# Perceiver block on Trainium2: GpSimd takes part of the closing sums, shared sums come earlier, the last load is cut in two

## The chip, the core and the metric

The kernel runs on one core of a Trainium2 chip (trn2). The metric is the device time of one execution in microseconds (us); the median of several runs counts. Beside it there is one profiled execution with its trace, from which all durations of single instructions come. The engines are named as in the profile: PE (TensorE, matmuls; PEld is its weight load), DVE (VectorE), ACT (ScalarE), POOL (GpSimd) and SP (SyncE, which here issues most DMAs).

## What is computed

x is a tensor of 64 sequences of 32 rows with 256 features: 2048 rows. Six residual layers follow each other: windowed cross-attention to a context, causal self-attention, a quantised linear layer, full cross-attention, a gated mixer with a short convolution, and a mixture of experts. Only the end of the last one matters here. Cut to that:

```python
flat = layernorm(x).reshape(2048, 256)
probs = softmax(flat @ router_w + router_b)              # 8 experts
topk_probs, topk_idx = top_k(probs, 2)                    # two experts per row
shared_out = gelu(flat @ sw1 + sb1) @ sw2 + sb2
h1 = gelu(einsum('td,edh->teh', flat, rw1) + rb1)
expert_out = einsum('teh,ehd->ted', h1, rw2) + rb2
out = x + shared_out + sum over the two chosen e of topk_probs[t, e] * expert_out[t, e]
```

## The kernel before

x stays in SBUF in four tiles `x0` to `x3`, one for each group g of 512 rows. A group has NT = 4 subtiles t of 128 rows, so a tile is 128 partitions x 4 x 256 numbers (float32). The tiles collect the residual sum in place, and the result is stored from them.

`mixture()` (line 1621) does the last layer. It routes the rows, and runs 20 turns over tiles of rows sorted by expert: POOL gathers rows of y by an indirect DMA (`gather`, line 1815), PE and ACT compute the hidden layer, PE the output, DVE adds the expert's bias, and POOL scatters the result by an indirect DMA to a DRAM buffer `r_rows` (`outputs`, line 1948, the DMA at line 1964). `r_rows` holds, for both choices `which` of each row, that expert's output in the row's own place.

After the last scatter the closing stage begins (line 2015 onward):

- **Loads.** SP loads `r_rows` back in eight DMAs of 512 KB, in the order g = 0..3, and within a group `which` = 0, 1 (lines 2020 to 2022). They wait for the last scatters.
- **Weights.** `weigh(g)` (line 2033): ACT multiplies subtiles of r in place by the routing weights `pw`, one instruction of 128x256 each. `by_scalar` (line 2028) says which subtiles ACT takes: all four for `which` = 1; for `which` = 0 only t = 2 and 3, but all four in group 3; and none of the last load (g = 3, `which` = 1).
- **Sums.** `sum_up(g)` (line 2039): where ACT has scaled, DVE adds two subtiles of r to x in one `tensor_tensor` of 128x512. Elsewhere DVE multiplies and adds in one `scalar_tensor_tensor` of 128x256 per subtile. After the second choice of a pair of subtiles, SP issues the store of this pair, 256 KB: eight stores in all.
- **The shared expert.** `fill_outputs(n)` (line 1115, which steps through `shared_outputs`, line 1068) lets PE compute the shared expert's output for n subtiles into PSUM, and `settle()` (line 1089) lets DVE add what is ready to x, a pair of subtiles (128x512) at a time. The results `ps_so` alternate between two PSUM banks, so the matmuls of a pair wait until DVE has read the pair before the last one. At the start of the closing stage four pairs are left: both of group 2 and both of group 3.

Engines take their instructions in program order, and the order of the closing stage is this:

```python
        for g in range(NG):
            weigh(g)
        fill_outputs(2)
        settle()
        sum_up(0)
        for g in range(1, NG):
            fill_outputs(2)
            settle()
            sum_up(g)
```

So one shared pair is settled ahead of each group's sums: group 2's first pair ahead of group 0's sums, group 2's second ahead of group 1's, group 3's first ahead of group 2's, and group 3's second ahead of group 3's own. POOL has nothing to do in this stage after its last scatter. All instructions issued through the helper of line 107 bear that line in the profile; matmuls bear line 119.

The functions:

Of the kernel before, what the change touches and what calls it, by code (L numbers as in the profile page):

```python
# [12 lines left out]
ALU = mybir.AluOpType  # L13
# [7 lines left out]
NG, NT = 4, 4  # L21
# [44 lines left out]
def perceiver_kernel(ctx: ExitStack, tc: tile.TileContext, a: dict, out: bass.AP):  # L66
# [32 lines left out]
    class InOrder:  # L99
# [12 lines left out]
    vector, scalar, gpsimd, sync = (  # L112
        InOrder(e) for e in (nc.vector, nc.scalar, nc.gpsimd, nc.sync)
    )
# [974 lines left out]
    def settle(n=None):  # L1089
        for _ in range(len(owed) if n is None else n):  # L1090
            owed.pop(0)()

    def by_halves(unit, places):
        places = iter(places)
        begun = []

        def fill(n):
            left = round(2 * n)
            while left:
                if begun:  # L1100
                    finish(begun.pop())
                    left -= 1
                    continue
                half = unit(*next(places), left == 1)
                next(half)
                if left == 1:
                    begun.append(half)
                else:
                    finish(half)
                left -= min(left, 2)  # L1110

        return fill

    fill_hidden = by_halves(shared_hidden, [(g, c) for g in range(NG) for c in range(4)])
    fill_outputs = by_halves(shared_outputs, [(g, t) for g in range(NG) for t in range(NT)])
# [505 lines left out]
    def mixture():  # L1621
# [393 lines left out]
        r_view = r_rows[: 2 * NB * S].rearrange("(w g t p) d -> g p w t d", w=2, g=NG, p=P)  # L2015
        whole = sb.tile([P, 4, NT, D], F32, tag="kb0", name="r")
        r = [(whole[:, 0], whole[:, 1]), (whole[:, 2], whole[:, 3])]
        r_ = ring(sb, *wide[0:4])
        r += [tuple(r_([P, NT, D], "r") for _ in range(2)) for _ in range(2)]
        for g in range(NG):  # L2020
            for which in range(2):
                sync.dma_start(out=r[g][which], in_=r_view[g, :, which])

        def weight(g, which, t):
            at = which * nt + g * NT + t
            return pw[:, at : at + 1]

        def by_scalar(g, which):
            if g == NG - 1 and which == 1:
                return ()  # L2030
            return range(NT) if which or g == NG - 1 else range(2, NT)

        def weigh(g):
            for which in range(2):
                for t in by_scalar(g, which):
                    rows_t = r[g][which][:, t, :]
                    scalar.activation(rows_t, rows_t, AF.Copy, scale=weight(g, which, t))

        def sum_up(g):
            for which in range(2):  # L2040
                for t0 in range(0, NT, 2):
                    if t0 in by_scalar(g, which):
                        x = xs[g][:, t0 : t0 + 2, :]
                        vector.tensor_tensor(x, x, r[g][which][:, t0 : t0 + 2, :], ALU.add)
                    else:
                        for t in range(t0, t0 + 2):
                            x = xs[g][:, t, :]
                            vector.scalar_tensor_tensor(
                                x, r[g][which][:, t, :], weight(g, which, t), x, ALU.mult, ALU.add
                            )  # L2050
                    if which == 1:
                        sync.dma_start(
                            out=out_view[g][:, t0 : t0 + 2], in_=xs[g][:, t0 : t0 + 2]
                        )

        for g in range(NG):
            weigh(g)
        fill_outputs(2)
        settle()
        sum_up(0)  # L2060
        for g in range(1, NG):
            fill_outputs(2)
            settle()
            sum_up(g)

    out_view = out.rearrange("(g t p) d -> g p t d", g=NG, p=P)
    mixture()
    attention.close()

# [151 lines left out]
```

## Time and profile before

| what | value |
|---|---|
| median of 3 runs | 887.53 us (887.43 to 887.73) |
| the profiled execution | 888.15 us, its span 886.4 us |
| PE busy in the span | 851.0 us (96%) |
| DVE, ACT, POOL busy | 576.1, 438.5, 513.9 us |
| first load of r issued | 865.41 us into the span |
| last instruction of DVE ends | 883.15 us |
| closing stage, from the first load to the end | 21.0 us |
| plain adds x<-x,r on DVE | 11 of 128x512, 685 ns mean |
| weighted adds x<-r,w,x on DVE | 10 of 128x256, 478 ns mean |
| shared sums x<-ps_so,x on DVE in the stage | 4 of 128x512, 685 ns mean |
| scalings r<-r,w on ACT | 22 of 128x256, 496 ns mean |

Times in the trace are counted from the span's start. A group of instructions bears a mean duration; consecutive instructions on one engine overlap a little, so the distance from start to start is shorter than the duration. DMAs appear twice: as an issue on SP's queue, and as packets on the 16 DMA engines. The chain of waits follows instructions on engines; it ends with the last of these, and a transfer that lands after it is not part of it.

### The profile page before, as it was taken

What the parts mean: (1) busy time and instruction counts of PE and PEld (TensorE: products, weight loads), DVE (VectorE), ACT (ScalarE), POOL (GpSimd) and SP (SyncE); (2) the same over time, 40 slices, a digit from 0 to 9 for tenths busy, and PEclk for the clock granted to TensorE, in tenths of its full rate; (3) what the DMA queues carried; (4) which work ended last, traced back from release to release, by engine and by line L of the source; (5) the groups of instructions that cost most, each with busy time, mean ns of one, the idle gap of its engine ahead of it and who ended that gap; (6) DMA issues with size and microseconds to landing.
All of it is one profiled execution on the core that took longest, in us unless ns stands there. A gap on an engine that the chain in (4) does not pass through costs nothing. (4 is left out here: it accounts for less than half of the span.)

```text
span 886.4 us, 22890 instructions
## 1 busy us (share of the span) xinstructions
PE 851.0 (96%) x8729; PEld 586.9 (66%) x8729; DVE 576.1 (65%) x1692; ACT 438.5 (49%) x1135; POOL 513.9 (58%) x1004
## 2 busy tenths in 40 slices
PE   7989999999999999999999999999999999999995
PEld 3566666665466666666666665666667568888894
DVE  6888777896777576885778756866766861111116
ACT  2756667674654555565445645575652323222224
POOL 4677777785774657575575754685651254555430
PEclk9999999999999999999999999999999999999999
DMA  6564433553110111110111101120010046777768
GB/s 216 146 164 119 120 92 96 143 138 104 54 55 24 34 54 55 55 55 2 55 54 56 55 1 55 55 73 25 3 36 2 24 169 219 232 232 232 220 191 290
DMA packets 66926, 88.77 MB, mean 100 GB/s; under 512 B 32480, under 2 KB 50688, under 8 KB 64768
## 3 DMA queue, kind: packets, MB, share of 16 engines
q1 hardware_dynamic: 62592, 76.95, 28.9%
q0 software_dynamic: 3456, 9.44, 3.2%
q8 instruction: 69, 1.13, 0.5%
q10 hardware_dynamic: 768, 0.92, 0.4%
q14 instruction: 41, 0.34, 0.1%
HBM read 65.78 MB, written 13.11 MB: 89 GB/s over the span
## 5 line engine op out<-in xcount | busy, mean ns | idle before, releaser
L107 ACT ACTIVATE e<-e,xnm 128x257 f32<-128x257 f32 x256 | 127.2, 499 | 43.7 <-DVE xnm L107 40.4
L119 PE MATMUL ps_k<-ct,w_w_l1x 128*128 128x512 f32 x256 | 122.8, 602 | 1.1 <-ACT yT L107 0.5
L107 POOL TENSOR_SCALAR e<-e,xsm 128x256 f32<-128x256 f32 x256 | 123.4, 500 | 0.0
L107 DVE CUSTOM_DVE_ANT_0 e<-ps_s,mask 128x257 f32<-128x257 f32 x256 | 93.5, 421 | 43.3 <-PE ps_s L119 43.1
L119 PE MATMUL ps_v<-w_w_l1x,ct 128*128 128x256 f32 x512 | 121.1, 379 | 0.0
L122 PE MATMUL ps_t<-cst,e 128*128 128x128 f32 x640 | 101.7, 281 | 2.3 <-DVE eT L107 2.0
L119 PEld LDWEIGHTS ps_v<-w_w_l1x,ct 128*128 128x128 f32 x512 | 93.4, 190 | 10.8 <-ACT y L107 0.2
L107 DVE COPY eT<-ps_t 128x512 f32<-128x512 f32 x124 | 85.1, 686 | 23.4 <-PE ps_t L122 23.3
L107 ACT ACTIVATE kT<-ps_k,vec 128x512 f32<-128x512 f32 x64 | 44.0, 687 | 97.9 <-PE ps_k L119 96.4
L107 POOL TENSOR_TENSOR x<-x,rows 128x256 f32<-128x256 f32 x96 | 70.0, 747 | 28.2 <-DVE y L107 24.9
L107 ACT ACTIVATE hTr<-ps_h,w 128x256 f32<-128x256 f32 (+1 forms) x80 | 31.4, 450 | 110.3 <-issue 89.4
L122 PEld LDWEIGHTS ps_t<-cst,e 128*128 128x128 f32 x640 | 71.4, 140 | 20.1 <-DVE eT L107 4.8
L107 DVE TENSOR_TENSOR og<-ps_o,b 128x512 f32<-128x512 f32 (+1 forms) x20 | 12.8, 638 | 105.6 <-PE ps_o L119 105.6
L119 PEld LDWEIGHTS ps_k<-ct,w_w_l1x 128*128 128x128 f32 x256 | 44.6, 190 | 42.0 <-issue 34.1
L1964 POOL DMA_INDIRECT r_rows<-og,lv x36 | 35.5, 986 | 60.8 <-DVE og L107 55.9
L119 PE MATMUL ps_h<-ygT,w 128*128 128x256 f32 (+1 forms) x320 | 67.2, 364 | 0.0
L107 ACT COPY v<-ps_v 128x512 f32<-128x512 f32 x80 | 46.4, 581 | 41.1 <-PE ps_v L119 40.7
L107 POOL TENSOR_TENSOR last<-e,xsm 128x4 f32<-128x4 f32 x64 | 15.3, 238 | 88.6 <-DVE xsm L107 87.1
L119 PE MATMUL ps_o<-w,hTr 128*128 128x256 f32 x288 | 65.3, 379 | 0.0
L119 PEld LDWEIGHTS ps_h<-ygT,w 128*128 128x128 f32 x320 | 56.0, 194 | 6.4 <-issue 0.2
L119 PEld LDWEIGHTS ps_o<-w,hTr 128*128 128x128 f32 x288 | 54.4, 190 | 7.2
L107 ACT ACTIVATE kb<-kT,cst 128x256 f32<-128x256 f32 x96 | 45.4, 512 | 23.8 <-POOL kT L107 23.7
(225 smaller groups left out, 1671.4 us busy)
## 6 DMA issues: line engine op xcount, KB each, us to landing
ct<-in_ctxT SPq DMA_DIRECT2D x16, 1024.0 KB
w<-in_ew SPq DMA_DIRECT2D x20, 514.0 KB
w<-in_ew SPq DMA_DIRECT2D x20, 512.0 KB
far<-part SPq DMA_DIRECT2D x126, 64.0 KB
v_rows<-v SPq DMA_DIRECT2D x16, 256.0 KB
vb<-v_rows SPq DMA_DIRECT2D x64, 64.0 KB
r<-r_rows SPq DMA_DIRECT2D x8, 512.0 KB
b<-in_eb SPq DMA_DIRECT2D x20, 128.0 KB
```

Of the source, the lines that this page charges most:

```text
L107: ins = getattr(self.engine, name)(*args, **kw)
L119: return kept(nc.tensor.matmul(ps, **args))
L122: return kept(nc.tensor.transpose(ps, src, eye))
L1964: wrote = nc.gpsimd.indirect_dma_start(out=r_rows, out_offset=bass.IndirectOffsetOnAxis(ap=write_i[:, at : at + 1], axis=0), in_=o[:, i, : ...
```

## The change

```diff
         for g in range(NG):
             for which in range(2):
-                sync.dma_start(out=r[g][which], in_=r_view[g, :, which])
+                for t0 in range(0, NT, 2 if g == NG - 1 and which == 1 else NT):
+                    ts = slice(t0, t0 + 2) if g == NG - 1 and which == 1 else slice(0, NT)
+                    sync.dma_start(out=r[g][which][:, ts], in_=r_view[g, :, which, ts])
...
                     if t0 in by_scalar(g, which):
                         x = xs[g][:, t0 : t0 + 2, :]
-                        vector.tensor_tensor(x, x, r[g][which][:, t0 : t0 + 2, :], ALU.add)
+                        eng = gpsimd if which == 0 and t0 == 2 else vector
+                        eng.tensor_tensor(x, x, r[g][which][:, t0 : t0 + 2, :], ALU.add)
...
         for g in range(NG):
             weigh(g)
-        fill_outputs(2)
+        fill_outputs(4)
         settle()
-        sum_up(0)
-        for g in range(1, NG):
-            fill_outputs(2)
-            settle()
+        for g in range(NG):
             sum_up(g)
+            if g < 2:
+                fill_outputs(2)
+                settle()
```

Three things are in it.

1. In each group, the plain add of the first choice's subtiles 2 and 3 (128x512) moves from DVE to POOL: four adds. DVE's add of the second choice to the same subtiles now waits for POOL. In group 3, where the second choice is not scaled by ACT, it is the weighted add of subtile 2 that waits.
2. Both shared pairs of group 2 are now settled ahead of group 0's sums, group 3's first pair after group 0's sums, and group 3's second pair after group 1's. The order of PE's matmuls stays as it was.
3. The last load (g = 3, `which` = 1) becomes two loads of 256 KB, of subtiles 0 and 1 and of subtiles 2 and 3. SP issues nine loads and then the eight stores as before. The weighted adds of subtiles 0 and 1 need only the first half.

On DVE four instructions fewer are issued, on POOL four more, on SP one more; ACT and PE have the same.

## The prediction

> **What bounds the end now.** Only the last 25 us of 886.4 are touched, so I read the chain of waits for that stretch first, then the timeline of VectorE (DVE), ScalarE (ACT) and the DMA issues, then the busy time by stages.
>
> ```profile
> by line: DVE x L107 0.5%; issue 0.1%; DVEq L2217 0.0%; DVEq L107 0.0%
> ...
> 880.88 1.08 DVE x L107 x2
> 881.96 0.40 DVEq L2217
> 882.36 0.79 DVE x L107 x2
> ```
>
> The chain says "DVE, adds into x", up to 883.15. But the span ends at 886.4: 3.2 us follow that the chain does not show.
>
> ```profile
> 865.41 6.98 SPq L107 DMA_DIRECT2D r<-r_rows  x8
> ...
> 872.61 10.94 SPq L107 DMA_DIRECT2D out<-x  x8
> ...
> 876.70 3.38 ACT L107 ACTIVATE r<-r,w 128x256 f32<-128x256 f32 x8 [0.30 <-DMA r<-r_rows]
> 877.09 0.87 DVE L107 SCALAR_TENSOR_TENSOR x<-r,w,x 128x256 f32<-128x256 f32 x2
> 877.88 1.89 DVE L107 TENSOR_TENSOR x<-x,r 128x512 f32<-128x512 f32 x3
> 879.68 0.68 DVE L107 TENSOR_TENSOR x<-ps_so,x 128x512 f32<-128x512 f32 x1
> 880.28 1.28 DVE L107 TENSOR_TENSOR x<-x,r 128x512 f32<-128x512 f32 x2
> 881.49 1.67 DVE L107 SCALAR_TENSOR_TENSOR x<-r,w,x 128x256 f32<-128x256 f32 x4
> ```
>
> DVE works without a gap to 883.15. A 128x512 add follows the next after 0.60 us (1.89 for three is 2 x 0.60 + 0.69), a weighted 128x256 add after 0.39.
>
> ```profile
> 868.00:872.00 4.00, 4.00 (x20) 3.53 (x19) 1.69 (x4) 1.96 (x5) 0.00 (x0) 1.00 1.10 365
> ...
> 876.00:880.00 4.00, 1.75 (x9) 1.19 (x7) 4.00 (x8) 3.70 (x9) 0.00 (x0) 1.00 1.09 367
> 880.00:882.00 2.00, 0.00 (x0) 0.00 (x0) 2.00 (x5) 0.08 (x1) 0.00 (x0) 0.99 1.09 384
> ...
> 883.00:884.00 1.00, 0.00 (x0) 0.00 (x0) 0.15 (x1) 0.00 (x0) 0.00 (x0) 0.50 0.75 249
> ```
>
> The last two columns are the DMA engines' busy share and GB/s: full from 868 to 882, with a dip only at 883. So there is a second bound, nearly as late as DVE. By the DMA queue's completions in the trace, the eight loads of r land from 869.36 to 879.78, about 1.5 us apart, and the eight stores at 880.42, 881.08, 881.71, 882.38, 883.04, 883.72, 884.55, 885.32. The first store was issued at 872.61 and landed at 880.42, just behind the last load: the queue works in order, 0.66 us per store. Only the last two stores wait for DVE: the eighth was issued at 883.18 and landed 2.14 us later. The program's end follows 1.05 us after that.
>
> **The floor.** If DVE were infinitely fast, stores 7 and 8 would follow the sixth at 0.66 each: 883.72 + 1.32 = 885.04, against 885.32. Whatever is taken off DVE can gain 0.28 us, 0.03% of the time. More is not to be had unless the loads get faster.
>
> **The change, part by part.**
>
> (1) *Four 128x512 adds leave DVE*: 4 x 0.60 = 2.40 us off its queue. This is the gross gain, of which the floor lets 0.28 through.
>
> (2) *They go to GpSimd (POOL).* Its row for such an add:
>
> ```profile
> L107 POOL TENSOR_TENSOR near<-near,cst x28: 1269/1278/1301, 29.2 to 187.5; 128x512 f32<-128x512 f32 x28
> ```
>
> So 1.27 us each, starting 0.08 after ACT's last scaling (the smallest gap in these rows). POOL's last scatter, queued ahead, ends at 863.83. ACT finishes the scaled pair at 870.35 (group 0), 873.45, 876.40 and 880.08 (group 3). Undisturbed, the adds are done at 871.7, 874.8, 877.75 and 881.43. The DVE add that waits for each comes at 872.68, about 875.6, 878.4; these waits cost nothing. In group 3 the weighted add of tiles 2 and 3 must wait for 881.43.
>
> (3) *The adds do not run beside DVE for free.* Early in this trace:
>
> ```profile
> 20.93 0.15 DVE L107 TENSOR_TENSOR sq<-r 128x4 f32<-128x4 f32 x1
> 21.09 1.26 POOL L107 TENSOR_TENSOR kT<-near,far 128x512 f32<-128x512 f32 x1 [0.40 <-DVE sq L107]
> 21.11 1.26 DVE L107 SCALAR_TENSOR_TENSOR sq<-sq,ve 128x4 f32<-128x4 f32 x1
> ...
> 22.41 0.16 DVE L107 SCALAR_TENSOR_TENSOR rn<-sq,r 128x4 f32<-128x4 f32 x1
> ```
>
> A 4-column operation of DVE, worth 0.16, took 1.26: it stood still while POOL added. With operations of the size in question:
>
> ```profile
> 688.36 1.58 POOL L107 TENSOR_TENSOR x<-x,rows 128x256 f32<-128x256 f32 x2 [0.71 <-ACT y L107]
> 688.53 1.69 DVE L107 SCALAR_TENSOR_TENSOR conv<-yT,vec,conv 128x248 f32<-128x248 f32 x2
> ```
>
> Each of these two weighted adds ended 0.27 after the POOL add beside it (690.22 against 689.94), where alone it takes 0.48. Both operands of these DVE operations lie in SBUF, as in the adds into x. The shared sums read PSUM; rows of that kind (part from ps_qk, ps_x into x) keep their 0.75 and 0.68 beside POOL, so I let them run.
>
> The Trainium skill, SBUF — State Buffer, section "Who interferes with whom", says that a VectorE instruction with two SBUF inputs and a GpSimd instruction that reads SBUF exclude each other, and that the second "fully blocks" until the first finishes. The 0.27 above is softer than this at the seam: by the rule the sum below would be +0.78, by the row -0.18.
>
> Now the DVE queue of the changed program, in its order, with the row's 0.27:
> - Shared sums ahead: group 2's second one at 869.06 (its matmuls end then), so the first weighted adds begin at 869.66, not 869.38. It is recovered at once: the next DVE add waits for ACT until 871.88, as before. Group 0's POOL add (870.5 to 871.75) lies in that gap.
> - Group 1: POOL 873.53 to 874.80. The two weighted adds, due at 873.89, end at 875.07 and 875.46; plain adds start at 875.38 and 875.98, the last shared sum at 876.58. Its matmuls follow group 3's first ones without the 1.55 us that TensorE waited at 874.03, and end by 875.9.
> - Group 2: POOL gets in at 876.6, to 877.87. Weighted adds end at 878.14 and 878.53; plain adds at 878.45 and 879.05; group 3's one plain add at 879.65.
> - Group 3: POOL 880.25 to 881.52. The weighted adds end at 881.79, 882.18, 882.57 and 882.96; if DVE's first of them gets ahead of POOL, the end is the same within 0.05.
>
> The eighth store goes out at 883.00, not 883.18: it lands at 885.14, the floor being 885.04. Of the 2.40 us, group 1 gives back 0.7, group 2 0.5, group 3 1.1: this is where the gain goes.
>
> (4) *The last load in two halves.* Same bytes. One more issue on SP: an issue of a load took 0.39 to 1.4 us there, mostly held by the full queue; it delays the first store's issue, which has no way to move before 879.8 anyway. The first half lands some 0.7 us ahead of 879.78, so at 879.1: group 3's first weighted adds are free from then, but DVE is there at 880.25 in any case. Worth nothing; at worst a gap of 0.1 between halves, at best stores' pace (0.66 per half instead of 0.74), 0.15. No wait of SP is new on the path: each store also waits for a load's landing, now one load later, and the eighth for the second half at 879.8, long past.
>
> The Trainium skill, DMA: Bandwidth & Descriptors, section "Anatomy of one DMA — SWDGE (gpsimd) path", gives each DMA about 2.0 us of fixed cost beside its bytes. Paid in sequence, that would put the second half and every store 2 us later, 889.5 in all; the stores' spacing of 0.66 in this trace speaks against it.
>
> **Sum.** Profiled execution: 888.15 in all, span 886.4; the median of the runs shown is 887.53, and I apply the difference to that. 887.53 - 0.18 = **887.35 us**.
>
> **Rivals.**
> - *Full exclusion* (the 21.11 row: the DVE operation waits the whole add and then takes its whole time, and POOL too waits for DVE's whole operation): three times some 0.3 later. By the same list the eighth store goes out at 883.96: +0.78, **888.3**. For it: that 1.26. Against it: the 0.27 of equally large operations.
> - *No blocking at all*: POOL's group 3 add ends at 881.43, two weighted adds behind it at 882.36; the floor of 885.04 decides: -0.28, **887.25**. Also what comes if the relief is real and the queue hides it. Rows at 21.1 and 688.5 speak against it.
> - *Slower: GpSimd closes late.* In the trace POOL's closing drain lasts to 869.79, 5.96 after its last scatter ended at 863.83; nothing shows why. Today it has 16 us to spare. Now POOL's last add ends at 881.52. If the drain again takes 5.96 after it, POOL is done at 887.48, SP's at 885.53 no longer decides: +1.95, **889.5**. It decides from 4.0 us on. Against it: POOL's drain at the program's start, after memsets, took 0.16, and the long one may belong to the scatters alone.
> - *Faster by more than 0.2%* would need 1.8 us off a queue that is full; I see no way.
>
> **Chances.** Forecast with no blocking beside it (887.1 to 887.7): 0.57. Full exclusion and mixtures up to 888.4: 0.30. Late close: 0.08. Rest 0.05, of which 0.02 faster, 0.02 slower. A measurement of this kernel can tell about 0.2% (1.8 us) from no change. So: faster 0.02, within 0.88, slower 0.10. The range goes from the floor with faster halves and the runs' spread (-0.28 - 0.15 - 0.1) to full exclusion with 0.1: 887.0 to 888.4; the late close is left out.
>
> **What would show it.** Right: DVE's weighted adds in groups 1, 2 and 3 at about 1.1 us instead of 0.48 where a POOL add lies beside them; TensorE's wait at 874.03 gone; DVE's last add near 882.96; the last store some 2.1 us behind its issue; DMA share full to 882 and the dip at 883 smaller. Wrong: POOL adds that start well after ACT's scaling or last over 1.3; DVE's last add after 883.5; a span that ends over 1.2 us after the last store (the drain); loads that land later than 879.8.

## The result, and the profile after

The changed kernel takes 889.88 us (median of 22 runs), the kernel before 887.72 in the runs beside it: 2.16 us more, a ratio of 1.0029 with a 95% interval of 1.0019 to 1.0039. It is slower, and the time lies outside the range that was given. Single runs scatter (885.90 to 891.01 before, 887.36 to 895.04 after). In the profiles of these two kernels and of the five variants below, the long part ahead of the closing stage, which none of them touches, ends anywhere from 862.99 to 866.88. So I read the two profiles from the issue of the first load of r (865.41 before, 864.07 after), where the closing stage begins:

| us after the first load's issue | before | after |
|---|---|---|
| DVE's last sum ends | 17.74 | 17.80 |
| the last store has landed | 19.91 | 20.01 |
| SP has seen everything land | 20.12 | 20.16 |
| POOL's last instruction ends | -1.58 | 16.33 |
| POOL's closing drain ends | 4.38 | 22.30 |
| the program ends | 20.96 | 23.16 |

Of the loss of 2.20 us, 0.10 had come up by the last store; it was the time behind that store that grew, from 1.05 to 3.15 us. The chain of waits of the changed kernel does not show it; it ends on DVE again, at 881.87:

```profile
by line: DVE x L107 0.3%; issue 0.2%; DVEq L2220 0.1%; DVEq L107 0.0%
...
879.35 1.09 issue
880.45 0.63 DVEq L2220
881.08 0.79 DVE x L107 x2
```

The busy time by stages of the changed kernel (the last two columns are DMA share and GB/s) does:

```profile
876.00:880.00 4.00, 0.00 (x0) 0.00 (x0) 3.87 (x7) 2.77 (x7) 1.59 (x2) 0.65 1.09 371
880.00:882.00 2.00, 0.00 (x0) 0.00 (x0) 1.87 (x4) 0.00 (x0) 0.40 (x1) 0.50 0.81 285
...
883.00:884.00 1.00, 0.00 (x0) 0.00 (x0) 0.00 (x0) 0.00 (x0) 0.00 (x0) 0.50 0.65 216
884.00:887.20 3.20, 0.00 (x0) 0.00 (x0) 0.00 (x0) 0.00 (x0) 0.00 (x0) 0.50 0.00 0
```

From 884.1 to 887.2 nothing moves: no engine computes, no byte is under way. The waits of SP's queue give this idle time a name. Before, in the last 10 us:

```profile
SPq L2217 <- DMA out<-x: 1.2, 2, 0.7
SPq L2217 <- PEq L2217: 0.7, 2, 0.5
```

After:

```profile
SPq L2220 <- PEq L2220: 2.9, 2, 2.3
SPq L2220 <- DMA out<-x: 1.1, 2, 0.8
```

The columns are total, count and the longest, in us. The line is the program's end, where all engines meet, and the longest wait went from 0.5 to 2.3. "PEq" is only the name that the view infers: at such a meeting it can't tell who was late. The sequencers' own records in the trace can. They hold three drains of POOL (a drain is the instruction that waits until the engine has nothing left); the longest is the closing one. Before and after:

```profile
L2217 POOLq DRAIN  x3: 45/113/7162, 862.6 to 886.1; - x3
L2220 POOLq DRAIN  x3: 45/113/7381, 879.0 to 887.0; - x3
```

The three numbers are the shortest, the median and the longest in ns. Before, the closing drain ran from 862.63 to 869.79; after, from 878.99 to 886.37, 5.98 us past the end of POOL's last add (880.40). Every other engine was ready by 884.24.

The sums themselves went almost as on the list:

```profile
872.15 1.28 POOL L107 TENSOR_TENSOR x<-x,r 128x512 f32<-128x512 f32 x1 [1.83 <-ACT r L107]
...
872.59 1.52 DVE L107 SCALAR_TENSOR_TENSOR x<-r,w,x 128x256 f32<-128x256 f32 x2
...
875.10 1.52 POOL L107 TENSOR_TENSOR x<-x,r 128x512 f32<-128x512 f32 x1 [1.67 <-ACT r L107]
...
876.01 1.28 DVE L107 SCALAR_TENSOR_TENSOR x<-r,w,x 128x256 f32<-128x256 f32 x2
...
879.03 1.37 POOL L107 TENSOR_TENSOR x<-x,r 128x512 f32<-128x512 f32 x1 [2.41 <-ACT r L107]
879.32 2.55 DVE L107 SCALAR_TENSOR_TENSOR x<-r,w,x 128x256 f32<-128x256 f32 x4
```

Two weighted adds take 0.87 undisturbed; beside POOL's adds they took 1.52 and 1.28, and the last four 2.55 instead of 1.67.

### The profile page after: what moved, and what is told of

Read it like the earlier page. It is cut to its first block, busy times and chain, and to the rows that moved or that the text cites. A ratio compares the mean times of both kernels' runs of the same rounds, so it can differ in the third digit from the quotient of the medians.

```text
span 887.2 us, 22893 instructions
## 1 busy us (share of the span) xinstructions
PE 850.0 (96%) x8729; PEld 587.2 (66%) x8729; DVE 576.5 (65%) x1688; ACT 438.5 (49%) x1135; POOL 518.2 (58%) x1008
## 5 line engine op out<-in xcount | busy, mean ns | idle before, releaser
L107 POOL TENSOR_TENSOR x<-x,rows 128x256 f32<-128x256 f32 x96 | 70.0, 747 | 28.5 <-DVE y L107 24.9
```

Of the source, the lines that this page charges most:

```text
L107: ins = getattr(self.engine, name)(*args, **kw)
```

## The experiments

Theory A: GpSimd's closing drain ends 5.97 us after its last instruction, whatever that is, and the program can't end sooner. Theory B, its rival: the adds on POOL hold up DVE's sums and the stores. Lines that begin with + or - are against the kernel that each paragraph names; "stage" is the time from the first load's issue to the end, from the profiled run.

**Only groups 0 to 2 on POOL** (against the changed kernel):

```diff
-                        eng = gpsimd if which == 0 and t0 == 2 else vector
+                        eng = gpsimd if which == 0 and t0 == 2 and g < NG - 1 else vector
```

> The changed kernel, but group 3's add of subtiles 2 and 3 stays on DVE; POOL keeps those of groups 0 to 2. Theory A (GpSimd's closing drain ends 5.97 us after its last instruction, and the program can't end before it): POOL's last add ends some 12.5 us after the first load's issue, its drain at 18.5, ahead of SP's at 20.1; the loss of 2.2 us is gone, ratio to before 0.9995 to 1.0005, the stage from the first load's issue to the end 20.7 to 21.0 us. Theory B (the adds on POOL hold up DVE's sums and so the stores): three quarters of the loss stay, +1.6 us, stage 22.6.

Measured: ratio to before 1.0000 (95% interval 0.9983 to 1.0016; the brackets below are such intervals too), 887.30 us. The loss is gone with one of four adds. POOL's last add ended at 13.26, its drain 5.98 later at 19.24, ahead of SP, and the meeting at the end is as short as before:

```profile
SPq L2220 <- DMA out<-x: 1.3, 2, 0.6
SPq L2220 <- PEq L2220: 0.7, 2, 0.5
```

The stage was 21.55, longer than expected: in this profile the third load landed at 7.92 instead of 6.96 us, and everything behind it in the queue moved along; the last store landed at 20.56, the end followed 0.99 later. That late load stands in the profiles of the next two kernels too (7.72, 7.30) and, less, in the last of the five (7.23), not in those of before (6.96) and after (6.92). Why is open.

**Only group 3 on POOL** (against the changed kernel):

```diff
-                        eng = gpsimd if which == 0 and t0 == 2 else vector
+                        eng = gpsimd if which == 0 and t0 == 2 and g == NG - 1 else vector
```

> The changed kernel, but only group 3's add goes to POOL; the other three stay on DVE. Theory A: the whole loss is there, ratio 1.002 to 1.003, stage 23 to 23.5 us (POOL's one add ends 16.3 to 16.8 us after the first load's issue, plus 5.97, plus 0.85). Theory B: a quarter of it, +0.5 us, stage 21.5.

Measured: ratio 1.0025 (1.0013 to 1.0037), 890.04 us, stage 23.43. POOL's one add ended at 16.60, the drain at 22.58. The whole loss hangs on this add:

```profile
SPq L2220 <- PEq L2220: 2.9, 2, 2.3
SPq L2220 <- DMA out<-x: 1.1, 2, 0.8
```

**No add on POOL** (against the changed kernel):

```diff
-                        eng = gpsimd if which == 0 and t0 == 2 else vector
+                        eng = vector
```

> The changed kernel with all four adds back on DVE: what is left is the shared sums ahead and the last load in two halves. Both theories: within 0.3 us of before (ratio 0.9995 to 1.0005, stage 20.8 to 21.2); if it is slower by more, the order of the shared sums or the cut load has a part in the loss.

Measured: ratio 1.0009 (0.9996 to 1.0022), 887.87 us, stage 20.77, just under what was expected: no difference that can be told. But DVE, with all adds its own, ended its last sum at 17.25, where it took until 17.80 with POOL's help and 17.74 before:

```profile
876.00 0.88 DVE L107 SCALAR_TENSOR_TENSOR x<-r,w,x 128x256 f32<-128x256 f32 x2
876.78 3.10 DVE L107 TENSOR_TENSOR x<-x,r 128x512 f32<-128x512 f32 x5
879.79 1.67 DVE L107 SCALAR_TENSOR_TENSOR x<-r,w,x 128x256 f32<-128x256 f32 x4
```

Eleven instructions without a gap, none stretched. So in these profiles the shared sums ahead, with the cut load, gain DVE 0.49 us, and the four adds on POOL cost it 0.55. Of the 0.49 only 0.13 reaches the last store, which landed at 19.78: the last three stores landed 0.67 us apart (18.44, 19.11, 19.78), so here the queue decided and no longer DVE.

**The kernel before, and one tiny instruction on POOL at the end** (against the kernel before, in `sum_up`):

```diff
+                    if which == 1 and (g, t0) == (3, 2):
+                        tiny = small.tile([P, 4], F32, tag="tiny", name="tiny")
+                        gpsimd.tensor_tensor(tiny, xs[g][:, t0 + 1, 0:4], xs[g][:, t0 + 1, 0:4], ALU.add)
```

> The kernel before, with one more instruction: behind DVE's very last sum, POOL adds 4 columns of x to themselves into a scratch tile that nobody reads. No sum and no store waits for it. Theory A: POOL's last instruction ends some 18.1 us after the first load's issue instead of long before it, so the drain ends at 24.1 and the program at 24.9: +3.9 us, ratio 1.0044. Theory B: nothing, stage 20.96, ratio 1.000.

Measured: stage 24.88, against 24.9 expected; DVE's last sum at 17.76 and the last store at 19.99, as before. The ratio is 1.0066 (1.0042 to 1.0091), 892.47 us; the 1.0044 expected lies just inside. An add of four columns, which took 0.20 us and for which nobody waits, costs 3.9 us of the stage:

```profile
882.98 0.20 POOL L107 TENSOR_TENSOR tiny<-x 128x4 f32<-128x4 f32 x1 [19.43 <-DVE x L107]
```

```profile
SPq L2220 <- PEq L2220: 4.6, 2, 4.0
```

**The same, behind group 2's last sum** (the condition is `(g, t0) == (2, 2)`):

> The kernel before, with POOL's scratch add of 4 columns behind DVE's last sum of group 2 instead of its very last sum. It should end some 14.6 us after the first load's issue. Theory A (a tail of 5.97 us behind GpSimd's last instruction): drain ends at 20.6, SP's at 20.1, so the tail decides by only 0.5 us: stage 21.4 to 21.5 us, ratio 1.0006. Theory B (work on POOL slows the sums): nothing, stage 20.96.

Measured: POOL's add ended at 14.67, its drain at 20.65, the stage was 21.50; ratio 1.0006 (0.9992 to 1.0020), which by itself tells nothing. With the runs at 13.26 (nothing lost), 16.33, 16.60 and 18.04 this is a threshold with a slope of one: by as much as POOL's last instruction ends after 14.15 (SP's 20.12 minus 5.97), the stage grows: by 0.54, 2.20, 2.47 and 3.92 in the four runs past that point, where 0.52, 2.18, 2.45 and 3.89 follow from it.

**What makes the drain so long?** Seven small kernels, one profiled execution of each, compute no layer: they load x, double it with DVE and store it, and differ in what POOL does (DVE also adds in a tile that POOL has cleared or gathered, where there is one). The core of the three with a gather and an add, GATHERS being 1, 16 and 72:

```python
for n in range(GATHERS):
    nc.gpsimd.indirect_dma_start(out=got[:, n % 8], out_offset=None, in_=a["x"],
        in_offset=bass.IndirectOffsetOnAxis(ap=at[:, 0:1], axis=0))
...
nc.gpsimd.tensor_tensor(xs[3][:, 0:2], xs[3][:, 0:2], xs[3][:, 0:2], ALU.add)
```

> A small kernel by itself, which computes no layer: it loads x, doubles it with DVE and stores it; POOL's one instruction of its own is a memset of 128x1024 early on. What is the tail between POOL's last instruction and the end of its closing drain? If every closing drain has it: 5.97 us. If it comes from GpSimd's loaded arithmetic or from its indirect DMAs: under 0.3 us, as at the program's start (0.16).

> The same small kernel; POOL's one instruction is an add of 128x512 near the end, and there is no indirect DMA in it. If the tail belongs to any last instruction or to arithmetic on POOL: 5.97 us. If it needs an indirect DMA in the program: under 0.3 us.

> The same small kernel; POOL's one instruction is an indirect DMA early on, no arithmetic on POOL. If the tail belongs to any last instruction or to indirect DMAs: 5.97 us behind it. If it needs arithmetic on POOL: under 0.3 us.

> A small kernel again, no layer computed: one indirect gather by POOL early on, then DVE doubles x, then POOL adds 128x512 at the very end with DVE idle. Tail between the end of that add and the end of POOL's closing drain: 1.8 us or more if one indirect DMA anywhere in the program is enough; about 0.15 us if the tail grows with the number of indirect DMAs (5.97 over the 72 of the large kernel is 0.08 each); 0.07 if it belongs to the number of POOL instructions.

> The same with 16 gathers. One is enough: the same tail as with one gather. Grows with the indirect DMAs: 1.3 to 1.4 us. Number of POOL instructions: about 0.2 us.

> The same with 72 gathers, as many indirect DMAs as the large kernel has. Grows with the indirect DMAs: 5.9 to 6.0 us. One is enough: as with one gather. Number of POOL instructions: 0.5 us.

> The same without a gather, but with 300 earlier adds of 128x256 on POOL. Number of POOL instructions: 1.8 to 2 us (300 of the large kernel's 1000). Indirect DMAs in any form: 0.07 us.

| POOL's work | indirect DMAs | last instruction | tail of the drain behind it, us |
|---|---|---|---|
| memset | 0 | memset | 0.07 |
| one add | 0 | add | 0.07 |
| 300 adds, add | 0 | add | 0.07 |
| gather, add | 1 | add | 0.16 |
| 16 gathers, add | 16 | add | 1.39 |
| 72 gathers, add | 72 | add | 5.97 |
| one gather | 1 | gather | 1.85 |
| the large kernel before, after and in all five variants | 72 | scatter or add | 5.96 to 5.98 |

The tail is 0.07 us and 0.082 for every indirect DMA that POOL has issued in the program: 0.07 + 72 x 0.082 = 5.97, and for 16 it gives 1.38. That the DMAs lie far back does not help: in the kernel of 72 the last gather ended at 100.42, the add at 120.79, the drain at 126.76, and SP waited for it:

```profile
SPq L64 <- PEq L64: 3.0, 2, 2.5
SPq L64 <- DMA out<-x: 2.7, 1, 2.7
```

POOL's arithmetic and the number of its instructions have no part in it. Nor has the kind of indirect DMA: 36 gathers and 36 scatters in the large kernel give the tail of 72 gathers. But all of them move 128 rows of 1 KB, so these runs can't tell a cost for each DMA from one for each row or packet, and no DMA that POOL issues without an index list was tried. The one gather with nothing behind it does not fit the line; there the drain ended at 13.55, when DVE had just begun (13.50) the add that waited for the gather's data, so it may have waited for the landing. That was not tried further. What the engine does in the tail is open; the runs show its length alone.

## Why the prediction was wrong

- **The bound and the floor** held for the stores. With no add on POOL, DVE ended 0.49 us earlier than before and the last store landed only 0.13 earlier, at the queue's pace. In the changed kernel the last store followed DVE, 2.15 us behind its issue, as in the kernel before (2.14). What the floor left out is that the program's end waits for POOL too.
- **The blocking** held. In groups 1, 2 and 3 the first weighted add ended 0.28 us after POOL's add, where 0.27 was taken from the early row. The Trainium skill, SBUF — State Buffer, section "Who interferes with whom", calls what the two share "an exclusive lock". Here the blocked add ended 0.28 us behind POOL's recorded end, less than the 0.48 that it takes alone. POOL was held up too: its adds took 1.27 to 1.52.
- **The forecast for DVE** was 17.55 for its last sum (882.96), and 17.80 was measured: the term that was mis-sized is the step from the weighted to the plain adds in groups 1 and 2. With the add of subtiles 2 and 3 gone to POOL, DVE's next plain add goes into the very subtiles that the weighted adds ahead of it have just written. It began 0.09 us after their end, where the list let it overlap by 0.08: 0.17 each time, and 0.25 of it in all was left at the end. It was not ACT that held it: in group 1 ACT had scaled these subtiles by 873.42, the weighted add ended at 874.11, and DVE's wait ahead of the plain add ended at 874.15. With no add on POOL, the add of subtiles 2 and 3 stands between the two, and the overlap is there in both groups. The last store landed at 20.01 instead of 19.73: a quarter of a microsecond, not the loss.
- **The cut load** was worth nothing, as said: the halves landed 0.72 and 0.69 us behind what landed ahead of each, 1.41 together, where the whole load took 1.42 before. The 2.0 us that the Trainium skill, DMA: Bandwidth & Descriptors, section "Anatomy of one DMA — SWDGE (gpsimd) path", gives as fixed cost is for DMAs issued through GpSimd, and SP issues these. No such cost is paid in sequence here: the last store landed 2.15 us behind its own issue, but the halves and the stores behind them landed some 0.7 us apart.
- **The step that failed is the choice among the rivals**, "GpSimd closes late". The sum let SP's queue alone set the program's end and so put the drain behind POOL's last add at nothing; it measured 5.98 us and ended 2.14 us after SP was ready. The rival as written had this right: its price (forecast +1.95, measured +2.16 to +2.20), its mechanism (the drain ends 5.97 after the last add), and that a tail of 4.0 us would be enough (POOL's last add ended 3.84 ahead of SP). It got a chance of 0.08 on two arguments, and both were wrong. "POOL's drain at the program's start took 0.16": at that point no indirect DMA had been issued, so that row says nothing on a drain after 72 of them. "The long one may belong to the scatters alone": it goes by the number of indirect DMAs, gathers as well as scatters, but it is paid behind whatever comes last, 18 us later too. The one row that was like the case, the 5.96 at the end of this very program, should have had the most weight, and no other row spoke of it. The range left that case out, and the measured time lay 1.5 us above it.

## What to carry to other kernels

Before you give an engine work near the end of a program, look in the profile for how long its closing drain ran on behind its last instruction, and add that length to the end of the new work; an idle engine is not a free one. Here the tail is 0.082 us per indirect DMA (of 128 rows) that GpSimd issued, 5.97 us in all, so GpSimd's last instruction has to end that much ahead of the last store's landing. An engine that adds beside DVE from the same memory may give no relief: with four adds of 0.60 taken off DVE, its last sum came 0.55 later than with all of them on it (one profile of each). And where the chain of waits ends earlier than the span, read what lies behind it first.

## What was not expected of the hardware

- The tail of the drain: 0.07 us without indirect DMAs, 0.16, 1.39 and 5.97 with 1, 16 and 72.
- In the small kernel with one add on POOL, that add was ready at 19.74 while DVE made 128x1024 adds without a pause. It ended at 23.96, after 4.22 us, 0.89 after DVE's last one (23.07); with DVE idle it takes 1.03. DVE had one instruction running and two behind it at 19.74; none of them was stretched, and by the end of POOL's add it was let in at neither seam between them. The timeline of DVE shows the stretch as one:

```profile
16.17 6.89 DVE L43 TENSOR_TENSOR x<-x 128x1024 f32<-128x1024 f32 x6
```
